# Differential attention of two batches taken out of its own stage: one beside the last exps, one beside the experts

## The chip, the cores and the metric

The kernel runs on one core of one Trainium2 chip. The metric is the device time of one execution in microseconds (us). The kernel before took 1091.72 us, the median of three runs (1090.41 to 1093.3).

## The reference, cut to what matters

The input is x with 8 batches of 512 tokens of width 128, in float32. Two blocks follow each other. Each normalizes its rows (layer norm), feeds the normalized rows to an attention and, in parallel, to a second layer, and adds both to x.

- Block 0: causal attention with 16 heads of width 8, beside a soft mixture of experts (64 slots for each of 8 experts).
- Block 1: *differential attention* beside a transformer layer of its own. That layer has a small causal attention over the batch index (the eight tokens at one position), a router that picks the best two of 8 experts for each token, at most 1280 tokens for each expert in order of arrival, and the experts (128 to 512 to 128 with GELU).

```
# differential attention of one batch, xn its normalized rows
q1, q2 = split(xn @ w_q12);  k1, k2 = split(xn @ w_k12);  v = xn @ w_v
a = softmax(q1 k1^T / sqrt(128)) - lam * softmax(q2 k2^T / sqrt(128))
out = a @ v;  out = out / rms(out) * (1 - 0.8)
x += out + transformer_layer(xn)
```

The order of arrival makes the router serial over the batches: the place of a token in its expert's list (its *rank*) counts all earlier tokens of that expert.

## The kernel before, in words

Names: a tile is 128 partitions wide; a batch is 4 tiles of 128 rows (NI is 4). PE multiplies matrices, DVE is VectorE, ACT is ScalarE, POOL is GpSimd, SP issues plain transfers. Each engine works its own queue in order. The order of PE, DVE, ACT and POOL follows the order in which the program is written out: `in_order` (L230) chains each engine's instructions up to the experts in that order.

The program has four stages.

1. **The soft experts of block 0** (L513 to L578), and then a start of the attention.
2. **The attention loop of block 0** (L1185 to L1228). A step `e_` is called a *third* here: one third of the causal score tiles of one group of 4 heads, 96 thirds (N3) in all, 12 to a batch. A third's work has two halves. `m_head` (L1035) makes scores for the row maximum (PE line L1042, DVE line L1052); `e_head` (L1066) makes the scores again and ACT takes the exp (L1075, L1080). `m_head` runs AHEAD (8) thirds in front of `e_head`, so in the last 8 thirds there is only `e_head`. After each third POOL masks the exps (L1085) and PE multiplies them with the values (`av`, L1100). A batch ends with `out_att`, `out_T` and `out_x` (L1111 to L1140), which add the attention to x.
3. **Differential attention**, `diff(range(NB))` (L1334), one batch after the other: four projections (`diff_qk`, L1253), the values (`diff_v`), and for each of 4 row tiles two score matmuls with max and exp (`diff_scores`, L1277, L1281, L1282), their difference (`diff_both`, L1295), transposes (`diff_T`) and the product with the values (`diff_out`, L1311). `diff_end` scales the rows on DVE and adds them to x, and `store` writes the batch to the output.
4. **The experts** (L1398). For each expert SP loads its 1280 rows (L1400), PE transposes them (L1418), multiplies (L1428), ACT does the GELU (L1431), PE multiplies again (L1435), DVE scales (L1441), and POOL issues ten indirect transfers (L1446), each of which adds 128 rows to the output. The additions of an expert wait until all those of the expert before have landed.

**Leads.** The transformer layer's attention and router for batch b are a generator, `lead(b)` (L665), started when `out_x(b)` is done. `step_leads` (L1169) advances each open lead by at most one step in each *slot* (a quarter of a third, or one step of `diff`). A lead's chain is: layer norm (`ln_stats`, `ln_apply`), its projection (L690), b+1 query products on POOL, each summed on DVE (L722, L716), an exp, b+1 value products on POOL, each added on DVE (L751, L760), the output projection (L782), a second layer norm, the router (L812 to L851, small operations going to and fro between DVE and POOL), the ranks (L858 to L877), and 8 indirect transfers on POOL that put the rows into the experts' lists (*puts*, L903). A lead may not begin its query products before the lead in front of it is done with its values (`after("sc", s_ - 1)`, L703). All puts of all leads must have landed before the first load of an expert's rows (L1401).

**Ranks.** PE adds up 9 small matmuls in one tile (L858 to L868): the counts of earlier batches (`seen`), the tokens above in the same tile (`tri`, once for each of two choices), and the whole tiles before it (`ones`, six times).

The lists of steps 3 and 4 use different PSUM pools; in stage 3 tag "d" has 3 buffers for the scores and "t" has 3, in stage 4 "t" has 2 (L1392).

Of the kernel before, what the change touches and what calls it, by code (L numbers as in the profile page):

```python
# [18 lines left out]
P = 128  # L19
# [6 lines left out]
def kernel(ctx: ExitStack, tc: tile.TileContext, a: dict, out: bass.AP):  # L26
# [203 lines left out]
    def in_order(start, end=None):  # L230

        free = mybir.DependencyInfo(mybir.DependencyClass.NoSync, mybir.DependencyReason.DATA)
        last = {}
        for ins in list(nc.cur_bb.bb.instructions)[start:end]:
            if ins.engine in engines:
                if ins.engine in last:
                    tc.add_manual_dep(ins, last[ins.engine], free, reason="order of the trace")
                last[ins.engine] = ins.name

# [348 lines left out]
    seen = const.tile([P, NE], F32, name="seen")  # L588

    def routing_in():  # L590
# [5 lines left out]
        nc.gpsimd.memset(seen, 0.0)  # L596
# [38 lines left out]
    def ln_stats(name, rows):  # L635
        stt = small.tile([P, 4, 6], F32, tag="bn_st", name=f"st_{name}")
        mv = small.tile([P, 4, 2], F32, tag="bn_mv", name=f"mv_{name}")
        for k, r in enumerate(rows):
            dve.bn_stats(out=stt[:, k, :], in_=r)
            dve.bn_aggr(out=mv[:, k, :], in_=stt[:, k, :])  # L640
            yield 1, "dve"
# [23 lines left out]
    def lead(s_):  # L665
# [37 lines left out]
        yield from after("sc", s_ - 1)  # L703
        sc = wt("sc", [NI * H, NB])
# [15 lines left out]
        for t in range(n):  # L720
# [3 lines left out]
            if len(behind) > BEHIND:  # L724
                yield 1, "dve"
                sum_q(*behind.pop(0))
# [22 lines left out]
        for t in range(n):  # L749
# [8 lines left out]
            if len(behind) > BEHIND:  # L758
                yield 1, "dve"
# [51 lines left out]
        for i in range(NI):  # L811
# [39 lines left out]
        pool.tensor_scalar(out=hot[:, 1], in0=off, scalar1=0.0, scalar2=None, op0=ALU.is_equal)  # L851
        yield 3, "pe"
# [5 lines left out]
        nc.tensor.matmul(  # L858
            pr, lhsT=ones, rhs=seen.unsqueeze(1).to_broadcast([P, NI, NE]), start=True, stop=False
        )  # L860
        for k in range(2):
            nc.tensor.matmul(pr, lhsT=tri, rhs=hot[:, k].rearrange("p i e -> p (i e)"), start=False, stop=False)
        for k in range(2):
            for i in range(NI - 1):
                nc.tensor.matmul(
                    pr[:, (i + 1) * NE :], lhsT=ones,
                    rhs=hot[:, k, i].unsqueeze(1).to_broadcast([P, NI - 1 - i, NE]),
                    start=False, stop=(k == 1 and i == NI - 2),  # L868
                )
# [4 lines left out]
        new = rtile("new", (NE,))  # L874
        dve.tensor_reduce(out=new, in_=hot.rearrange("p k i e -> p e (k i)"), axis=AX.X, op=ALU.add)
# [11 lines left out]
        pool.tensor_tensor(out=seen, in0=seen, in1=new, op=ALU.add)  # L887
# [10 lines left out]
        yield 3, "pool"  # L898

        for i in range(NI):  # L900
            m = s_ * NI + i
            for k in range(2):
# [8 lines left out]
                yield 1, "pool"  # L911
# [4 lines left out]
    with ExitStack() as at:  # L916
# [226 lines left out]
        AHEAD = 8  # L1143
# [20 lines left out]

        leads = []
# [3 lines left out]
        def step_leads(slot_, pe_free, pool_free, more):  # L1169
            room[0] = min(room[0] + more, more)  # L1170
            spare[0] = min(spare[0] + more * SPARE, CAPA * more)
            for r in list(leads):
                if slot_ < r[1] or (r[2] == "pe" and not pe_free) or (r[2] == "pool" and not pool_free):
                    continue
                if r[2] == "dve" and room[0] <= 0 or r[2] == "act" and spare[0] <= 0:
                    continue
                if r[2] == "pool":
                    pool_free = False
                nxt = next(r[0], None)
                if nxt is None:  # L1180
# [4 lines left out]
        for e_ in range(-AHEAD, N3 + 4):  # L1185
# [13 lines left out]
            for n in range(4):  # L1199
# [20 lines left out]
                if e_ < 0:  # L1220
                    next(rest, None)
                step_leads(4 * e_ + n, n == 1, n < 3, ROOM)
# [6 lines left out]

        in_order(first)  # L1230


    with ExitStack() as l1b:
# [9 lines left out]
        wka = l1b.enter_context(tc.tile_pool(name="wka", bufs=2, reuse_waits="tile"))  # L1243


        ascale = D ** (-0.25)
        OUT = (1.0 - LAMBDA_INIT) * math.sqrt(D)
        dd = {}

        def diff_qk(b):  # L1250
            for n, (w, c) in enumerate((("wq1", 0), ("wk1", 0), ("wq1", 1), ("wk1", 1))):
                pq = psum_t(f"pqk_{b}_{n}")
                nc.tensor.matmul(pq, lhsT=l1p[w][:, c * D : (c + 1) * D], rhs=xnT[:, b], start=True, stop=True)  # L1253
                dd["qk", b, n] = o = wka.tile([P, T], F32, tag=f"qk1_{n}", name=f"qk1_{b}_{n}")
                nc.scalar.activation(o, pq, AF.Identity, scale=ascale if w == "wq1" else 1.0)
                yield

        def diff_v(b):
            pv = psum_t(f"pv1_{b}")
            for i in range(NI):  # L1260
                nc.tensor.matmul(
                    pv[:, i * D : (i + 1) * D], lhsT=xnT[:, b, i * P : (i + 1) * P], rhs=l1p["wv1"], start=True, stop=True
                )
            dd["v", b] = v = wka.tile([P, NI, D], F32, tag="v1", name=f"v1_{b}")
            nc.scalar.copy(v.rearrange("p i d -> p (i d)"), pv)

        def diff_scores(b, i):

            u = f"{b}_{i}"
            nm = small.tile([P, 2], F32, tag="nm", name=f"nm1_{u}")  # L1270
            dd["ex", b, i] = ex = wka.tile([P, 2, T], F32, tag="ex1", name=f"ex1_{u}", bufs=4)
            if i == 0:
                dd["sm", b] = small.tile([P, NI, 2], F32, tag="sm1", name=f"sm1_{b}")
            sm = dd["sm", b][:, i]
            for k in range(2):
                sc = psum_t(f"s1_{u}_{k}", "d")
                nc.tensor.matmul(  # L1277
                    sc, lhsT=dd["qk", b, 2 * k][:, i * P : (i + 1) * P], rhs=dd["qk", b, 2 * k + 1],
                    start=True, stop=True,
                )  # L1280
# [212 lines left out]
```

## Time and profile before

| what | value |
|---|---|
| median of 3 runs | 1091.72 us |
| the profiled execution | 1097.12 us |
| its span, first to last instruction | 1095.4 us |
| PE / DVE / ACT / POOL busy | 91% / 60% / 50% / 51% of the span |
| mean granted TensorE clock | 0.941 |
| last `out_x` of block 0 ends (start of stage 3) | 732.1 us into the span |
| first load of an expert's rows issued | 900.0 us |
| first transposes of an expert's rows on PE | 915.2 us |
| first addition to the output issued | 929.1 us |
| last addition issued | 1089.6 us |

The profiled execution is 1.7 us longer than its span and 5.4 us longer than the median. A row of the table by stretches has, after its bounds, the length of the stretch, then the busy time and the number of instructions of PE, of its weight loads, of DVE, ACT and POOL, then the granted clock of PE (1.00 is full), the busy share of the DMA engines and what they moved. Busy PE is not the same as fast PE: at a granted clock of 0.50 the same matmuls take about twice as long and still count as busy. In the timeline a bracket shows how long the engine had been idle before an instruction and what ended the idle time.

### The profile page before, as it was taken

How to read it: one execution, taken by the hardware profiler on the slowest of the kernel's cores; microseconds unless marked ns; L12 is line 12 of the kernel's file. 1: busy time of each engine (PE TensorE's matmuls, PEld its weight loads, DVE VectorE, ACT ScalarE, POOL GpSimd, SP SyncE). 2: the span in 40 equal slices, each digit the busy share in tenths (PEclk: the TensorE clock that was granted, in tenths of full speed). 3: DMA queues.
4: the chain of work that ended last, by engine and by line, in shares of the span. 5: the costliest groups of instructions: out<-in, count | busy, mean ns of one | idle time of the engine just before them, and what ended most of it. 6: DMA issues, size and time to landing. Idle time of an engine off the chain costs nothing.

```text
span 1095.4 us, 19018 instructions
## 1 busy us (share of the span) xinstructions
PE 1000.8 (91%) x6838; PEld 639.9 (58%) x6838; DVE 661.9 (60%) x2134; ACT 551.4 (50%) x1263; POOL 559.7 (51%) x761
## 2 busy tenths in 40 slices
PE   6889899989899999999999999788978987999992
PEld 3457556866455555555556555354655655777772
DVE  6734543287677887788878689437786754222220
ACT  3566348352456676667465654526554753222220
POOL 3201000202143527675876787875877351777776
PEclk8999899999799999999999899759998998999996
DMA  8630000000000000000000000050000013342312
GB/s 249 149 91 1 1 1 1 1 1 1 1 1 2 1 2 2 20 2 1 17 7 1 21 19 4 1 171 1 20 11 20 20 44 94 49 67 40 29 15 25
DMA packets 49311, 32.99 MB, mean 30 GB/s; under 512 B 12232, under 2 KB 44275, under 8 KB 49216
## 3 DMA queue, kind: packets, MB, share of 16 engines
q1 hardware_dynamic: 34832, 24.80, 8.4%
q0 software_dynamic: 13568, 6.70, 4.5%
q8 instruction: 54, 0.88, 0.3%
q14 instruction: 41, 0.34, 0.1%
q10 hardware_dynamic: 816, 0.26, 0.1%
HBM read 17.56 MB, written 17.07 MB: 32 GB/s over the span
## 4 chain that ended last, share of the span: by engine, by line
PE 73%; POOL 10%; DVE 9%; issue 4%; ACT 3%; DMA 2%; POOLq 0%; DVEq 0%; ACTq 0%; SPq 0%
PE se L1075 11%; PE sm L1042 7%; PE pem L1435 7%; PE po L1100 7%; PE phm L1428 6%; PE lg_d L302 3%; PE s L1277 3%; PE pe L477 3%; PE psl L346 3%; PE lg_c L302 2%; PE pq L962 2%; PE pf L379 2%; PE ph L451 2%; POOL xs L903 2%; DVE junk L1052 2%
## 5 line engine op out<-in xcount | busy, mean ns | idle before, releaser
L1052 DVE CUSTOM_DVE_ANT_0 junk<-sm,cmask 128x128 f32<-128x128 f32 (+3 forms) x512 | 249.6, 488 | 82.2 <-PE sm L1042 29.3
L1080 ACT ACTIVATE pt<-se 128x384 f32<-128x384 f32 (+1 forms) x384 | 186.5, 528 | 175.1 <-PE se L1075 102.2
L1042 PE MATMUL sm<-kj,qT 32*128 32x256 f32 (+3 forms) x1024 | 229.9, 485 | 4.3 <-ACT kj L629 2.7
L1075 PE MATMUL se<-q,kj 32*128 32x512 f32 (+3 forms) x1024 | 212.0, 484 | 3.8 <-DVE q L616 3.6
L1075 PEld LDWEIGHTS se<-q,kj 32*128 32x128 f32 x1024 | 101.2, 192 | 83.1 <-issue 26.7
L1446 POOL DMA_INDIRECT out_dram<-es,to x80 | 124.2, 1552 | 48.0 <-issue 22.5
L1085 POOL TENSOR_SCALAR_AFFINE_SELECT pt<-pt 128x512 f32<-128x512 f32 (+1 forms) x96 | 79.3, 826 | 128.2 <-ACT pt L1080 127.8
L1042 PEld LDWEIGHTS sm<-kj,qT 32*128 32x128 f32 x1024 | 111.5, 190 | 20.6 <-DVE mcol L1052 6.5
L1100 PE MATMUL po<-pt,vpad 128*18 128x512 f32 (+3 forms) x1024 | 92.9, 460 | 9.2 <-POOL pt L1085 9.2
L1431 ACT ACTIVATE hTm<-phm 128x1024 f32<-128x1024 f32 (+1 forms) x48 | 42.2, 881 | 109.5 <-PE phm L1428 105.0
L1435 PEld LDWEIGHTS pem<-w,hTm 128*128 128x128 f32 x640 | 77.1, 192 | 16.8 <-ACT hTm L1431 12.1
L1435 PE MATMUL pem<-w,hTm 128*128 128x128 f32 x640 | 81.2, 278 | 0.5 <-ACT hTm L1431 0.2
L1428 PE MATMUL phm<-xeT,w 128*128 128x512 f32 (+1 forms) x192 | 75.2, 523 | 2.3 <-DVE xeT L1420 2.3
L1441 DVE TENSOR_SCALAR es<-pem,wt 128x128 f32<-128x128 f32 x80 | 22.9, 345 | 89.9 <-PE pem L1435 85.2
L1282 ACT ACTIVATE ex<-s,nm 128x512 f32<-128x512 f32 x64 | 43.8, 687 | 65.9 <-DVE nm L1281 65.3
L903 POOL DMA_INDIRECT xs<-l_z,sput x64 | 66.1, 1033 | 17.2 <-issue 16.3
L508 POOL TENSOR_TENSOR x_all<-x_all,bo_bc 128x512 f32<-128x512 f32 x8 | 10.2, 1277 | 121.8 <-DVE xn L266 121.8
L1277 PE MATMUL s<-qk,qk 128*128 128x512 f32 x128 | 65.4, 630 | 5.0 <-ACT ex L1282 5.0
L1281 DVE TENSOR_REDUCE nm<-s 128x1 f32<-128x512 f32 x64 | 42.7, 682 | 20.0 <-PE s L1277 19.1
L1100 PEld LDWEIGHTS po<-pt,vpad 128*18 128x18 f32 x1024 | 21.0, 99 | 52.3 <-issue 21.6
L1311 PEld LDWEIGHTS po<-v,dT 128*128 128x128 f32 x256 | 35.2, 204 | 20.9 <-ACT sqj L1315 10.2
L1428 PEld LDWEIGHTS phm<-xeT,w 128*128 128x128 f32 x192 | 33.6, 191 | 23.1 <-issue 17.2
(264 smaller groups left out, 1906.4 us busy)
## 6 DMA issues: line engine op xcount, KB each, us to landing
xs<-cmask SPq DMA_DIRECT2D x1, 5280.0 KB
xe<-xs SPq DMA_DIRECT2D x8, 660.0 KB
x_all<-in_L_attn_x_dram SPq DMA_DIRECT2D x8, 256.0 KB, 4.2
w<-in_L_ffn_w_dram SPq DMA_DIRECT2D x1, 2048.0 KB, 9.1
w<-in_L_ffn_moe_w_dram SPq DMA_DIRECT2D x1, 2048.0 KB
out_dram<-x_all SPq DMA_DIRECT2D x8, 256.0 KB, 2.2
out_dram<-es,to POOLq DMA_INDIRECT x80
xs<-l_z,sput POOLq DMA_INDIRECT x64
```

Of the source, the lines that this page charges most:

```text
L302: nc.tensor.matmul(lg, lhsT=lhs(k), rhs=rhs, start=True, stop=True)
L903: put = nc.gpsimd.indirect_dma_start(out=xs, out_offset=bass.IndirectOffsetOnAxis(ap=sput[:, k, m : m + 1], axis=0), in_=z2[:, i], in_offs ...
L1042: nc.tensor.matmul(sc[:, o : o + w], lhsT=st["qT", b][rr, i * P : (i + 1) * P], rhs=st["k", b, j][rr, :w], start=True, stop=True,)
L1052: nc.vector.tensor_tensor_reduce(out=junk[:, :w], in0=sc[:, o : o + w], in1=cmask[:, 512 - w : 512], scale=-1.0, scalar=BIG, op0=ALU.add, ...
L1075: nc.tensor.matmul(sc[:, o : o + w], lhsT=st["k", b, j][rr, c * P : (c + 1) * P], rhs=st["q2", b, (g % G) // 2][rr, c * P : T], start=True ...
L1080: nc.scalar.activation(st["pt", g, k][:, r, :o], sc[:, :o], AF.Exp)
L1085: nc.gpsimd.affine_select(out=pt[:, :, :n, :P], in_=pt[:, :, :n, :P], pattern=[[0, 4], [0, n], [1, P]], compare_op=ALU.is_ge, fill=0.0, ba ...
L1100: nc.tensor.matmul(po[32 * r : 32 * r + 2 * PW, c * P : T], lhsT=vpads[b % 3][:, c, at_ : at_ + 2 * PW], rhs=pt[:, r, o : o + w], start=(c ...
L1277: nc.tensor.matmul(sc, lhsT=dd["qk", b, 2 * k][:, i * P : (i + 1) * P], rhs=dd["qk", b, 2 * k + 1], start=True, stop=True,)
L1428: nc.tensor.matmul(ph[:, k, :w], lhsT=w1_1[:, e, hc * P : (hc + 1) * P], rhs=xeT[:, :w], start=True, stop=True)
L1435: nc.tensor.matmul(pe[:, k * D : (k + 1) * D], lhsT=hT[:, hc, k * P : (k + 1) * P], rhs=w2_1[:, e, hc, :], start=(hc == 0), stop=(hc == NH ...
L1446: back = nc.gpsimd.indirect_dma_start(out=out_rows, out_offset=bass.IndirectOffsetOnAxis(ap=to[:, c : c + 1], axis=0), in_=es[:, c], in_of ...
```

## The change

It has six parts.

- **Ranks.** POOL adds the two choices (`both`) and keeps running counts for every tile (`seen` gets NT + 1 entries); PE then needs 2 matmuls for a batch in place of 9, and DVE one sum less.
- **AHEAD** goes from 8 to 9.
- **Leads in stage 3** take steps whose pause is one slot and whose kind is "act" (or "row", a new name for the layer norm's sums) together in one slot; and `sc` has two buffers, so that a lead's query products wait only for the lead two in front. "put" and "sum" are further names of kinds.
- **The early batch.** Batch 0's `diff` runs in the attention loop from third 88 on, one step in each slot, with tiles borrowed from the loop (`home`), and its products in SBUF. Its row tiles use two score buffers in turn.
- **The late batch.** Batch 7's `diff` runs in stage 4, two steps in each group of row tiles (three groups to an expert) of the first four experts, between the GELU and the second matmuls. Its x is stored before the experts; its attention is scaled in SBUF and added to the output by one POOL transfer of the whole batch after expert 4's additions, which it awaits and which expert 5's additions await.
- **Stage 3** keeps batches 1 to 6, and `behind` chains the experts' instructions on each engine behind the last one of stage 3.

```diff
-    seen = const.tile([P, NE], F32, name="seen")
+    seen = const.tile([P, NT + 1, NE], F32, name="seen")
...
-        yield from after("sc", s_ - 1)
-        sc = wt("sc", [NI * H, NB])
+        yield from after("sc", s_ - 2)
+        sc = wt("sc", [NI * H, NB], bufs=2)
...
+        both = rtile("both")
+        pool.tensor_tensor(out=both, in0=hot[:, 0], in1=hot[:, 1], op=ALU.add)
+        for i in range(NI):
+            m = s_ * NI + i
+            pool.tensor_tensor(out=seen[:, m + 1], in0=seen[:, m], in1=both[:, i], op=ALU.add)
         yield 3, "pe"
...
-        nc.tensor.matmul(
-            pr, lhsT=ones, rhs=seen.unsqueeze(1).to_broadcast([P, NI, NE]), start=True, stop=False
-        )
-        for k in range(2):
-            nc.tensor.matmul(pr, lhsT=tri, rhs=hot[:, k].rearrange("p i e -> p (i e)"), start=False, stop=False)
-        for k in range(2):
-            for i in range(NI - 1):
-                nc.tensor.matmul(
-                    pr[:, (i + 1) * NE :], lhsT=ones,
...
+        nc.tensor.matmul(pr, lhsT=ones, rhs=seen[:, ns].rearrange("p i e -> p (i e)"), start=True, stop=False)
+        nc.tensor.matmul(pr, lhsT=tri, rhs=both.rearrange("p i e -> p (i e)"), start=False, stop=True)
...
-        AHEAD = 8
+        AHEAD = 9
...
+        EARLY = (0,)
+        LATE = (NB - 1,)
+        APART = EARLY + LATE
...
+            if tag == "ex1":
+                t = wkp.tile([P, NG, S], F32, tag="sq", name=name) if i % 2 == 0 else wkp.tile([P, NI, 2 * H, S], F32, tag="qk", name=name).rearrange("p i h s -> p (i h) s")
...
+                sc = psum_t(f"s1_{u}_{k}", "d" if b not in APART else "t")
...
+            if b in APART:
+                nc.vector.tensor_copy(to, po)
...
                 nxt = next(r[0], None)
+                while nxt and nxt[0] == 1 and nxt[1] in at_once:
+                    nxt = next(r[0], None)
...
+                if e_ >= N3 - 8:
+                    if n % 1 == 0:
+                        next(early, None)
                 step_leads(4 * e_ + n, n == 1, n < 3, ROOM)
...
-        run = diff(range(NB))
+        run = diff(range(len(EARLY), LATE[0]))
...
-                step_leads(slot_, True, True, 9.0)
+                step_leads(slot_, True, True, 9.0, ('act', 'row'))
                 slot_ += 1
+        for b in LATE:
+            store(b)
         in_order(tail)
+        experts = len(nc.cur_bb.bb.instructions)
...
+        late = diff(LATE)
         for e in range(NE):
...
+                if e < 4:
+                    for _ in range(2):
+                        next(late, None)
                 pe = psum_o(f"pem_{e}_{c0}")
...
+            if e == 4:
+
+                for _ in late:
+                    pass
+                add = nc.gpsimd.dma_start(
+                    out=out[LATE[0]].rearrange("(i p) d -> p i d", p=P),
+                    in_=dd["po", LATE[0]].rearrange("p (i d) -> p i d", i=NI), accum_op=ALU.add,
+                )
+                for name in backs[e + 1]:
+                    tc.add_manual_dep(add.ins, name, sync, reason="a row is read and written by each addition")
+                backs[e + 1] = [add.ins.name]
+
+        behind(tail, experts)
```

The order in which the changed program issues its instructions: on PE the early batch lies between the scores of third 88 and those of third 94; on POOL, between the last mask and the last put, there are 32 puts, 15 query products, 16 value products and the small operations of leads 5 to 7; on ACT the table of functions is loaded 12 times more during experts 0 to 2, since the late batch's exps fall between the GELUs.

## Prediction

> **What bounds the kernel now.** I read the busy time by stretches first. Its columns are named under the table of the profile.
>
> ```profile
> 680.00:690.00 10.00, 7.81 (x74) 3.50 (x72) 8.91 (x28) 6.71 (x16) 7.41 (x13) 1.00 0.00 0
> 690.00:700.00 10.00, 6.17 (x52) 2.65 (x56) 2.73 (x3) 7.96 (x19) 9.75 (x12) 0.98 0.00 0
> 700.00:731.00 31.00, 28.49 (x134) 18.16 (x126) 11.33 (x30) 5.53 (x14) 20.49 (x35) 0.50 0.35 111
> 745.00:762.00 17.00, 13.42 (x56) 8.26 (x57) 11.61 (x24) 12.32 (x31) 5.13 (x8) 0.90 0.00 0
> 762.00:845.00 83.00, 73.32 (x354) 46.81 (x353) 60.70 (x130) 42.08 (x122) 68.52 (x97) 0.96 0.06 17
> 845.00:900.00 55.00, 53.81 (x277) 36.56 (x278) 37.16 (x93) 37.64 (x109) 24.12 (x47) 0.97 0.07 20
> 900.00:916.00 16.00, 8.98 (x51) 7.58 (x49) 7.26 (x27) 6.06 (x20) 1.95 (x4) 0.79 0.56 144
> 916.00:1076.00 160.00, 154.77 (x916) 116.46 (x916) 43.14 (x130) 43.85 (x51) 112.66 (x74) 1.00 0.29 41
> ```
>
> Four things are to be seen. At 690 to 700 PE is busy for 6.17 of 10 us, and from 700 to 731 it is granted half its clock: it looks busy, but does about half the work. From 762 to 845 POOL is the fullest that it gets in stage 3 (its short pauses between puts not counted). From 845 to 900 PE is the bound. From 916 to 1076 PE is full, and POOL too, once its pauses are counted.
>
> The timeline says what stands behind these rows: the stall ahead of the half clock, the stall at 900, and how the additions run.
>
> ```profile
> 699.70 0.63 PE L1100 MATMUL po<-pt,vpad 128*18 128x256 f32 x4 [3.28 <-POOL pt L1085]
> ...
> 904.70 0.17 DVE L1405 TENSOR_SCALAR first<-xe 128x10 f32<-128x10 f32 x1 [7.12 <-DMA xe<-xs]
> ...
> 929.11 1.67 POOL L1446 DMA_INDIRECT out_dram<-es,to  x1 [10.12 <-DVE es L1441]
> 931.09 1.57 POOL L1446 DMA_INDIRECT out_dram<-es,to  x1 [0.30 <-issue]
> ...
> 949.51 1.55 POOL L1446 DMA_INDIRECT out_dram<-es,to  x1 [2.02 <-DVE to L1412]
> ```
>
> The second line is an expert's first DVE instruction, queued ahead of differential work; it waits for the load and holds DVE for 7.12 us. The additions leave every 1.86 us (1.55 and a pause of 0.30), and between two experts POOL waits about 2 us for the landing: expert 1 starts at 949.5, expert 2 at 969.9, expert 5 at 1031.3, expert 7 at 1072.9, so 20.4 us an expert. PE needs 19.7 (its second matmuls start at 963.64, 1003.05 and 1042.46: 39.4 for two). Both limits nearly coincide.
>
> The list of waits, for stage 3 (735 to 915), names what PE waited for:
>
> ```profile
> PE dT_p L141 <- DVE ex L1295: 6.7, 4, 2.1
> PE po L1311 <- ACT sqj L1315: 6.4, 2, 6.0
> PE s L1277 <- ACT ex L1282: 5.0, 2, 4.0
> ```
>
> **The unit that is moved.** One batch of differential attention costs PE, at full clock by the chain of 855 to 900: 4 projections of 0.86, values 0.89, 8 scores of 0.86, 4 transposes of 0.63, 4 products of 0.89, together 17.3 us. DVE needs 11.4 us for it (42.7 + 26.1 + 9.5 + 4.8 + 7.9 us over 8 batches, lines L1281, L1295, L1292, L1291, L1328), ACT about 12.
>
> **Ranks: -5 us.** In the loop the 12 instructions of L865 take 1.32 us, 0.11 each; a batch has 18 (each matmul is two), the change leaves 4. That is 14 x 0.11 = 1.5 us of PE a batch. Four ranks lie in the loop ahead of third 88, where PE is busy for 20.00 us of 20 in most stretches: up to 6.2 us. What is late next is the POOL mask (PE waited 5.0 us for it between 280 and 680), and POOL gets four more operations a batch, of about 0.25 us with their gap (L887's kind). I take 5, bounds 0 and 6.2. The second buffer of `sc` moves POOL work forward in the loop; POOL is busy there for 5 to 19 us of 20, so I count nothing.
>
> **AHEAD 9: 0.** Four m_heads move from the loop to its start. PE: 4 x 0.23 us, hidden nowhere, but taken out of a full loop. DVE: 4 heads of 0.42 + 0.29 and gaps, 3.6 us at the start, where PE already waits for DVE (3.3 us for `q`). The new m_head is queued behind that `q`, not ahead of it. Bounds: -3.3 (the wait is covered) and +3.6 (all of DVE's work late).
>
> **The tail of the loop: +5.** Third 88 starts at about 680 and stage 3 at 732, 52 us. At full clock PE's work in it is 14 us (680 to 700) and about 16 of the 28.5 busy us at half clock (a set of 4 scores takes 0.86 us at 679 and 1.58 at 701), so 30. The early batch adds 17.3; the shorter rank takes 1.5, and the order of lead 5's projection puts another 1.5 into stage 3: 44.5 us of PE work. To this comes the closing chain (copy, transposes, division, transposes, copy, `pw`, addition: 0.59 + 0.63 + 0.78 + 0.63 + 0.59 + 1.2 + 0.7, 5 us) and I take 7 us for stalls: 57. The batch fills the time in which PE stood and ran slowly. Bounds: 48 (no stall) and 70 (half of the tail at half clock). One stall is built in: with two score buffers, the exp of row tile 2 waits on ACT for the transposes of row tile 0, and behind it in ACT's queue stand the block 0 exps, for whose buffers (7) PE waits next.
>
> [...]
>
> **Stage 3: -45.** Before it takes 183 us (732.1 to 915.2). After, two limits:
>
> - PE: 6 batches of 17.3 are 104, the PE work of leads 5 to 7 is 14 (transposes 0.63, `pp` 0.89, `pl` 0.79, the projection of lead 7 1.8, three ranks of 0.45): 118 us.
> - POOL, from the last mask to the last put: 32 puts each 1.28 us after the other (41), 15 query products of 1.25 (19), 16 value products of 1.14 (18), layer norm operations 10, additions 3 x 1.27 (4), routers 3 x 3.9, new counts 3 x 1.4, weights and slots 3 x 3.1, row scales of four batches 4 x 1.75: together 124 us, of which some 11 lie ahead of `out_x(7)`.
>
> So both stand near 115 us, and each waits for the other in its queue (a rank waits for POOL, products for DVE). DVE has about 6 x 11.4 plus leads, 110 us. From 762 to 845 POOL's busy time and its pauses between 16 puts (0.30 each) make 73 of 83 us, 88%. I take this rate: 124 / 0.88 = 141 us, less 11 is 130 to the last put. Then the load lands (4.6 us, 900.04 to the DVE line above) while PE ends batch 6, whose last work is late by the rank of lead 7; the row scales and the first rows' copy add 3: 138. The stall of 900 to 907 goes, since `behind` keeps the experts' DVE work behind stage 3. Bounds: 123 (124 - 11 and the load, no stalls) and 150 (80%).
>
> **Experts: +21.** The late batch gives PE 17.3 us over four experts: 19.7 + 4.3 = 24.0 us an expert, above POOL's 20.4. Expert 4's first addition comes 14 + 1.7 (two projections ahead) + 4 x 24.0 = 112 us after the stage's start; from the same event to the end the trace has 1095.4 - 1011.0 = 84.4 us. Then POOL is the bound again and nothing is made good. The new transfer of the whole batch stands between experts 4 and 5 with its own issue and landing; no row shows one. Below: one indirect issue and landing, 1.55 + 2.0; above: four of them, 4 x 1.86 + 2 = 9.4. I take 5, nearer to the single issue, because the plain store of as many bytes lands in 2.2 us. So 112 + 84.4 + 5 = 201 us, where it took 180.2. ACT's 12 loads of 1.28 us lie beside 3.6 us of second matmuls each time and cost nothing; if that cover fails, they are 15 us. PSUM tag "t" has two buffers here, which the late scores share with the rows' transposes; I count it in the upper bound. Bounds: +15 (PE's idle 5 us absorb a part) and +40.
>
> [...] The trace's loads last 1.28 us. [...]
>
> **Sum.** -5 + 0 + 5 - 45 (183 to 138) + 21 = -24 us. Against the profiled execution that is 1097.1 - 24 = 1073; the median lies 5.4 lower, so 1067 (1067.7).
>
> **Rivals.**
>
> - *Both limits of stage 3 are met and the clock holds.* Leads 5 to 7 now overlap, so POOL may never starve: stage 3 at 125, the tail at 50. Then -6 - 2 - 58 + 21 = -45: 1046. Against it: POOL waited in stage 3 for ACT and DVE (8.0 us for one exp). Chance 0.15.
> - *The early batch stalls the exps.* The ACT wait above empties PE, and the half clock stays: with 44.5 us of work, half of it at half clock, and the stalls, the tail takes 78 where I took 57. Then 1088 to 1090. For it: the clock did not return for 31 us before. Chance 0.12, and its spread reaches both sides of no change.
> - *Lead 7 keeps its length (slower).* In the trace it runs from 731 to its last put at 898.6, 167 us. If that is latency from step to step and not POOL's work, stage 3 cannot end before 167 + 8 = 175, and the late batch only lengthens the experts: -5 + 5 - 8 + 21 = +13, 1104. It decides from a lead of 155 us on. For it: the lead has over 40 steps that go to and fro between POOL and DVE. Against it: from 845 to 900 POOL was busy for 24 of 55 us and the lead followed PE's slots, of which there are now fewer. Chance 0.13.
>
> **How the numbers follow.** The forecast, 1055 to 1082, has 0.60. A change of 0.3% (3.3 us) is about what a measurement of this kernel can tell from none. Faster: 0.60 + 0.15 + 0.05 = 0.80; same 0.04; slower 0.03 + 0.13 = 0.16. The range, 1042 to 1092, holds the forecast, the fast case and most of the second rival, and leaves out the third.
>
> **What would show each step.** PE's granted clock between third 88 and stage 3 near 1.00 (the tail); from the last `pw` to the first transposes of an expert's rows 130 to 145 us, POOL busy over 85% (stage 3); no DVE wait for `xe` among differential work; second matmuls of experts 0 to 3 every 24 us and later every 19.7; the additions of experts 5 to 7 every 20.4 us; one gap of about 7 us ahead of expert 5's. The prediction is wrong if PE waits in stage 3 for lead 7's rank, if the tail shows 0.50, or if the big transfer holds POOL for over 10 us.

## The result, and the profile after

The changed kernel is slower. It took 1098.8 us, the median of 4 runs (1097.09 to 1101.7), where the kernel before took 1091.52 beside it (1090.41 to 1093.3): a ratio of 1.007, interval [1.0047, 1.0092]. The forecast was 1067, and 1042 to 1092 as its range.

The two profiled executions took 1097.12 (before) and 1097.09 us (after), so the traces differ by nothing where the medians differ by 7.3 us: the profiled execution of before lies 5.6 us above its median, that of after 1.7 below. Where in before's trace these 7 us lie isn't shown; its mean granted clock is 0.941, where 17 executions beside the first set of experiments had 0.944 to 0.949 at 1087.1 to 1095.0 us, so more time at half clock is the likeliest place. Two executions of the same code are up to 7 us apart at third 88 (673.2 in the kernel that is called neither below, 680.4 in rank_late57, which differs from it only later), so a few us of every time in the loop are chance. From there on, stages that two kernels share repeat within 2 us in most runs, and the reading goes by these.

I cut both traces at the same four points: the start of third 88's mask, the end of the last `pw` of block 0 (the product with the output weights, PE's last work in `out_x`), the end of the last put of lead 7, and the first transposes of an expert's rows.

| stage | before | after | forecast of the change | measured |
|---|---|---|---|---|
| up to third 88's mask | 681.3 | 674.1 | -5 | -7.2 |
| tail: third 88's mask to last `pw` | 50.1 | 59.8 | +5 | +9.7 |
| stage 3: last `pw` to first expert's rows | 183.9 | 160.7 | -45 | -23.2 |
| experts to the end | 180.2 | 200.8 | +21 | +20.6 |

The largest error is stage 3, by 22 us. In sum the stages were forecast at -24 us and came out at 0 between the two traces. The other 7 us of the miss are the forecast's last step, which took the median of the changed kernel 5.4 us below its profiled execution; it lies 1.7 above. The times of the stages are read from the traces at the starts and ends of these instructions. Busy time by stretches, of the changed kernel (columns as under the table of the profile before):

```profile
674.00:720.00 46.00, 45.99 (x248) 23.70 (x247) 21.22 (x45) 26.31 (x69) 21.42 (x42) 1.00 0.01 2
720.00:734.00 14.00, 8.31 (x53) 5.24 (x52) 3.40 (x9) 2.60 (x6) 11.51 (x17) 0.66 0.42 126
745.00:762.00 17.00, 13.73 (x43) 7.19 (x42) 15.02 (x34) 9.97 (x27) 10.97 (x16) 0.90 0.00 0
762.00:843.00 81.00, 67.62 (x307) 43.05 (x307) 61.74 (x123) 42.67 (x121) 69.73 (x102) 0.92 0.04 13
843.00:885.00 42.00, 37.32 (x187) 25.32 (x186) 24.41 (x64) 24.39 (x73) 23.55 (x47) 0.92 0.09 25
885.00:895.00 10.00, 5.05 (x22) 4.79 (x23) 2.17 (x7) 1.41 (x6) 2.13 (x7) 0.66 0.85 227
916.00:1076.00 160.00, 154.46 (x907) 115.74 (x906) 50.59 (x146) 63.06 (x85) 109.92 (x74) 1.00 0.29 40
```

The half clock of 700 to 731 is gone: PE is busy for all of 674 to 720 at 1.00, and only the end of the tail is slow (0.66 from 720 to 734). But PE is busy for 54.3 us in the two rows together, where I had counted 44.5 of work and some 2.5 for PE's part of the closing chain. In stage 3 POOL is as full as forecast only in the middle: 69.73 of 81 us, before its pauses between puts. From 745 to 762 it is busy for 10.97 of 17 us, and from 843 to 885 for 23.55 of 42. That last stretch is lead 7 alone. Its POOL timeline:

```profile
842.54 0.97 POOL L905 DMA_INDIRECT xs<-l_z,sput  x1 [0.30 <-issue]
...
849.55 0.23 POOL L127 TENSOR_SCALAR rs_l<-mv_l 128x4 f32<-128x4 f32 x1 [4.04 <-DVE mv_l L625]
...
860.26 0.24 POOL L835 TENSOR_TENSOR r_lg<-r_lg,r_most 128x32 f32<-128x32 f32 x1 [7.51 <-DVE cc L1232]
...
884.05 0.97 POOL L905 DMA_INDIRECT xs<-l_z,sput  x1 [0.30 <-issue]
```

After lead 6's last put (842.54) nothing of the leads but lead 7's output projection, second norm, router, rank and 8 puts is left for POOL, beside the row scales of two batches, and these steps go to and fro with DVE and PE: 42.5 us from the start of that put to the end of the last. And the list of waits for the same stage (735 to 905) shows what stood at the head of PE's queue:

```profile
PE prank L873 <- POOL seen L866: 9.5, 3, 4.1
PE dT_p L141 <- DVE ex L1236: 6.9, 3, 4.5
PE a1T_p L141 <- DVE l_at L625: 3.3, 1, 3.3
```

The rank is what the prediction named as a sign against it. In before PE waited 0.5 us for ranks in stage 3. At the end of the stage the expert's first DVE instruction no longer waits for its load, as forecast, but DVE waits all the same, for POOL's row scales (the first line below; the second is the expert's):

```profile
896.78 1.12 DVE L1279 SCALAR_TENSOR_TENSOR x_all<-po,ri,x_all 128x128 f32<-128x128 f32 x4 [7.50 <-POOL ri L129]
897.83 0.16 DVE L1449 TENSOR_SCALAR first<-xe 128x10 f32<-128x10 f32 x1
```

The experts went as forecast. The additions of experts 0 to 4 start at 910.2, 935.6, 959.6, 982.5 and 1007.1, 22.9 to 25.4 us apart and 24.2 in the mean, where 24.0 was forecast. The timeline of POOL between experts 4 and 5:

```profile
1023.76 1.55 POOL L1493 DMA_INDIRECT out_dram<-es,to  x1 [0.30 <-issue]
1027.08 1.39 POOL L1507 DMA_DIRECT2D out_dram<-po  x1 [1.77 <-DMA out_dram<-es,to]
1032.55 1.63 POOL L1493 DMA_INDIRECT out_dram<-es,to  x1 [4.08 <-DMA out_dram<-po]
```

From the end of the last addition (1025.31) to the next is 7.24 us, with the transfer of the whole batch between them. ACT's 13 loads of its table of functions in this stage, 1.28 us each, cost PE next to nothing: between 910 and 1090 PE waits 1.7 us for ACT in all.

### The profile page after: what moved, and what is told of

Same layout as the page of the kernel before. It is cut to its first block, busy times and chain, and to the rows that moved or that the text cites. A ratio compares the mean times of both kernels' runs of the same rounds, so it can differ in the third digit from the quotient of the medians.

```text
span 1095.4 us, 18827 instructions
## 1 busy us (share of the span) xinstructions
PE 991.4 (91%) x6726; PEld 604.5 (55%) x6726; DVE 669.5 (61%) x2134; ACT 569.1 (52%) x1275; POOL 567.7 (52%) x794
## 4 chain that ended last, share of the span: by engine, by line
PE 66%; POOL 13%; DVE 11%; issue 5%; ACT 3%; DMA 1%; POOLq 0%; DVEq 0%; ACTq 0%
PE se L1077 12%; PE pem L1482 6%; PE phm L1472 6%; PE po L1102 6%; PE sm L1044 4%; PE lg_d L311 3%; DVE junk L1054 3%; PE pe L486 3%; PE s L1218 3%; PE psl L355 3%; POOL xs L905 3%; PE pf L388 2%; PE pq L964 2%; PE lg_c L311 2%; PE ph L460 2%
## 5 line engine op out<-in xcount | busy, mean ns | idle before, releaser
L1077 PE MATMUL se<-q,kj 32*128 32x512 f32 (+3 forms) x1024 | 219.2, 472 | 4.0 <-DVE mcol L1054 3.5
L1077 PEld LDWEIGHTS se<-q,kj 32*128 32x128 f32 x1024 | 104.1, 186 | 91.2 <-DVE mcol L1054 24.3
L1044 PEld LDWEIGHTS sm<-kj,qT 32*128 32x128 f32 x1024 | 111.8, 190 | 24.5 <-DVE mcol L1054 10.2
L1102 PE MATMUL po<-pt,vpad 128*18 128x512 f32 (+3 forms) x1024 | 89.7, 446 | 10.5 <-POOL pt L1087 10.5
L1475 ACT ACTIVATE hTm<-phm 128x1024 f32<-128x1024 f32 (+1 forms) x48 | 41.6, 881 | 77.1 <-PE phm L1472 77.0
L905 POOL DMA_INDIRECT xs<-l_z,sput x64 | 66.9, 1046 | 16.6 <-issue 15.0
L1218 PE MATMUL s<-qk,qk 128*128 128x512 f32 x128 | 68.5, 645 | 4.0 <-ACT ex L1223 3.0
L1488 DVE TENSOR_SCALAR es<-pem,wt 128x128 f32<-128x128 f32 x80 | 22.9, 344 | 75.7 <-PE pem L1482 75.7
L1102 PEld LDWEIGHTS po<-pt,vpad 128*18 128x18 f32 x1024 | 20.6, 97 | 60.6 <-issue 21.1
L731 POOL TENSOR_TENSOR l_prod<-l_qkv 128x512 f32<-128x512 f32 x36 | 45.5, 1277 | 0.1
```

The lines of the kernel that those rows point to most:

```text
L905: put = nc.gpsimd.indirect_dma_start(out=xs, out_offset=bass.IndirectOffsetOnAxis(ap=sput[:, k, m : m + 1], axis=0), in_=z2[:, i], in_offs ...
L1044: nc.tensor.matmul(sc[:, o : o + w], lhsT=st["qT", b][rr, i * P : (i + 1) * P], rhs=st["k", b, j][rr, :w], start=True, stop=True,)
L1077: nc.tensor.matmul(sc[:, o : o + w], lhsT=st["k", b, j][rr, c * P : (c + 1) * P], rhs=st["q2", b, (g % G) // 2][rr, c * P : T], start=True ...
L1102: nc.tensor.matmul(po[32 * r : 32 * r + 2 * PW, c * P : T], lhsT=vpads[b % 3][:, c, at_ : at_ + 2 * PW], rhs=pt[:, r, o : o + w], start=(c ...
L1218: nc.tensor.matmul(sc, lhsT=dd["qk", b, 2 * k][:, i * P : (i + 1) * P], rhs=dd["qk", b, 2 * k + 1], start=True, stop=True,)
```

## The experiments

Twelve kernels were run, each five rounds against the kernel before, whose median was 1092.24, 1092.55 and 1093.88 in the three sets of four. The table has what all of them gave. Where an experiment is written as an edit, it is one of the changed kernel unless it names the kernel before. The ratio is to the kernel before, with its interval; "lead 7" is from the last `pw` to its last put, "rest" from there to the first transposes of an expert's rows, and the two make up stage 3. The stages are those of one execution each.

| kernel | batches in stage 3 | ratio | tail | lead 7 | rest | stage 3 | experts |
|---|---|---|---|---|---|---|---|
| before | 8 | 1 | 50.1 | 167.3 | 16.6 | 183.9 | 180.2 |
| after | 6 | 1.0070 [1.0047, 1.0092] | 59.8 | 151.1 | 9.6 | 160.7 | 200.8 |
| no_late | 7 | 0.9975 [0.9960, 0.9990] | 59.9 | 150.1 | 22.2 | 172.3 | 179.1 |
| no_early | 7 | 0.9941 [0.9923, 0.9959] | 40.1 | 149.2 | 22.2 | 171.4 | 199.3 |
| neither | 8 | 0.9907 [0.9889, 0.9924] | 37.9 | 150.7 | 38.7 | 189.5 | 178.8 |
| ranks_ahead | 8 | 0.9930 [0.9911, 0.9950] | 40.3 | 175.7 | 15.4 | 191.1 | 178.6 |
| ranks | 8 | 0.9987 [0.9968, 1.0007] | 45.2 | 170.4 | 16.7 | 187.0 | 178.9 |
| ahead9 | 8 | 0.9935 [0.9911, 0.9959] | 42.1 | 173.8 | 15.5 | 189.3 | 180.3 |
| early_fours | 6 | 0.9972 [0.9952, 0.9991] | 50.5 | 150.2 | 9.6 | 159.7 | 199.0 |
| best1 | 7 | 0.9881 [0.9859, 0.9903] | 50.4 | 150.1 | 22.2 | 172.3 | 179.1 |
| best1_nb | 7 | 0.9901 [0.9882, 0.9921] | 50.5 | 150.8 | 25.3 | 176.1 | 178.6 |
| lead7_short | 6 | 0.9911 [0.9889, 0.9932] | 52.2 | 129.5 | 22.9 | 152.4 | 199.7 |
| rank_later | 8 | 1.0146 [1.0117, 1.0176] | 52.6 | 154.7 | 38.8 | 193.5 | 182.3 |
| rank_late57 | 8 | 0.9935 [0.9912, 0.9958] | 40.2 | 150.9 | 37.5 | 188.3 | 181.1 |

### What the two moved batches are worth: no_late, no_early, neither

The theory after the result: stage 3 is as long as lead 7's chain, so a batch that leaves it gives back less than it costs elsewhere (L). The rival: the stage is the sum of its work, and gives back the full price of a batch (T).

```diff
# no_late
-        LATE = (NB - 1,)
+        LATE = ()
-        run = diff(range(len(EARLY), LATE[0]))
+        run = diff(range(len(EARLY), NB))
# no_early
-        EARLY = (0,)
+        EARLY = ()
# neither: both
```

> The changed kernel with the late batch put back as the seventh batch of stage 3 and no big transfer; everything else stays. Theory L (stage 3 of the changed kernel is as long as lead 7's chain of steps, 149.5 us from its start to its last put plus 10, and PE has some 40 us of slack in its 159 us): the batch put back costs stage 3 between 5 and 12 us, the experts give back 20.6, so 1098.8 - 20.6 + 8 = about 1086. Theory T (stage 3 is bound by the sum of its work, and a batch costs there what it costs elsewhere, 17 to 20 us): stage 3 near 177, 1096 to 1098.

> The changed kernel with the early batch put back as the first of seven in stage 3; everything else stays. The stretch from third 88 to stage 3 was 52 us in the kernel before and 63 in the changed one, so about 11 us come back there. Theory L: stage 3 grows by 5 to 12 us from 159, total 1093 to 1100, so that the early batch is worth about nothing. Theory T: stage 3 grows by 17 to 20 us, total 1104 to 1108.

> The changed kernel with all eight batches in stage 3; shorter ranks, AHEAD 9, the leads' new pace and the chaining of the experts behind stage 3 stay. Theory L: the two moves are a net loss. The loop keeps its 8 to 10 us, the tail returns to 52, the experts to 180, and stage 3 stays at 183 at most: 1080 to 1085. Theory T: stage 3 grows by 35 to 40 us to about 196, 1098.8 - 11 - 20.6 + 37 = 1104.

Measured: 1089.06, 1086.37 and 1081.64 us. No_late and neither lie nearer to L's totals, no_early lies below both. Without the two batches the rest of the change is a gain of 0.93%. The early batch alone (no_late against neither) costs 0.0068 x 1092 = 7 us, the late one alone (no_early) 4 us, both 18 us: 7 us more than the two by themselves, where each of these differences is known to some 3 us.

The stages say why, and both theories hold a part. The tail costs 20 to 22 us more with the early batch (59.8 against 40.1, 59.9 against 37.9), not the 11 that no_early's expectation took. The late batch costs the experts 20 to 22. Stage 3 gives 17 to 18 us back when the eighth batch leaves it (189.5 to 172.3 or 171.4), which is T, and 11 to 12 when the seventh does (to 160.7), which is L. The rows of the stretches up to lead 7's last put and behind it show how. First neither (eight batches), then no_late (seven), then after (six):

```profile
711.00:862.00 151.00, 124.06 (x539) 76.92 (x539) 110.17 (x233) 80.01 (x220) 111.31 (x172) 0.92 0.11 34
862.00:900.00 38.00, 35.62 (x197) 24.79 (x196) 24.57 (x59) 25.77 (x77) 5.34 (x14) 1.00 0.29 76
```

```profile
734.00:884.00 150.00, 125.28 (x535) 77.16 (x534) 108.42 (x232) 79.37 (x219) 110.46 (x171) 0.91 0.11 34
884.00:906.00 22.00, 19.61 (x122) 14.67 (x121) 14.49 (x35) 14.45 (x45) 4.16 (x11) 1.00 0.46 118
```

```profile
734.00:885.00 151.00, 126.33 (x556) 79.16 (x555) 109.96 (x235) 80.60 (x225) 111.40 (x171) 0.91 0.11 35
```

Up to the last put the three are the same: 150 us, in which PE is busy for 124 to 126 and POOL for 110 to 111. What is left of the batches then follows: 38 us and 22 us at full clock, or 10 us. The 10 us hold the load of the first rows and the last batch's end. The order of the program ties the batches to the leads' slots, and the leads take 150 us whether six or eight batches are to be fitted in. What sets these 150 us isn't told apart here, the leads' own steps or the PE work that the order puts between them.

PE's side of stage 3 can be split in three. The table has it by the busy time and by the stretches in which each trace grants half the clock (0.50). A set of four scores of one form takes 0.92 us in before at 679.40, at full clock, and 1.65 at 701.12, at 0.50. As an estimate from this, half of PE's busy time in these stretches is counted as lost, and the rest of the busy time is its work at full clock.

| kernel | batches | stage 3 | PE idle | lost at half clock | work at full clock |
|---|---|---|---|---|---|
| before | 8 | 183.9 | 22.7 | 11.5 | 149.7 |
| neither | 8 | 189.5 | 29.3 | 11.0 | 149.2 |
| no_late | 7 | 172.3 | 27.1 | 13.5 | 131.7 |
| after | 6 | 160.7 | 29.6 | 16.1 | 115.0 |

Each batch takes the 17 us of work with it that the prediction had priced. With the second one, PE's idle time and its loss at half clock grow by 5 us, and the stage gives back that much less.

### Which part brought the gain: ranks, ahead9, ranks_ahead

```diff
# ahead9: the kernel before with
-        AHEAD = 8
+        AHEAD = 9
# ranks: the kernel before with the shorter ranks of the change
# ranks_ahead: both; written from the changed kernel, with EARLY = (), LATE = (),
-        sc = wt("sc", [NI * H, NB], bufs=2)
+        sc = wt("sc", [NI * H, NB])
-                step_leads(slot_, True, True, 9.0, ('act', 'row'))
+                step_leads(slot_, True, True, 9.0)
# and without behind(tail, experts)
```

> The kernel before with the shorter ranks and AHEAD 9 alone: one sc buffer, the old pace of the leads, no chaining of the experts, all eight batches in stage 3. By the times of the masks these two parts are worth 8 to 10 us up to third 88, and the ranks of leads 4 to 7 another 4 to 6 us of PE work in stage 3: 1077 to 1083 against the 1091.5 of the kernel before. If the gain of the loop comes from the second sc buffer or the early batch instead, it stays within 1088 to 1092.

> The kernel before with the shorter ranks alone (AHEAD 8). Both together took 7.2 us off the time, 8 us up to third 88's mask and 10 us in the tail, where the half clock is gone. The instruction counts give the ranks 1.5 us of PE for each of the four in the loop: by them 1086 to 1088, with the half clock of the tail unchanged. If the ranks also end the half clock of the tail: 1076 to 1082.

> The kernel before with AHEAD 9 alone. The masks of thirds 6 to 36 come 3 us earlier in the changed kernel, ahead of any rank, so this part should be worth about 3 us: 1088 to 1090. If it is the ninth third that ends the half clock of the tail (fewer scores for PE to wait for there is no longer true, since m_heads end one third earlier and PE has less to do at the end): the clock would be no better, and the time 1090 to 1094.

Measured: 1085.07, 1090.48 and 1086.33 us. The shorter ranks can't be told from no change (0.9987, interval to 1.0007), AHEAD 9 gives 0.65%, both together 0.70%. None of the expectations had it that way: the ninth third is worth twice what I took at most, and the ranks a part of theirs. The tail of each of the three is 5 to 10 us shorter than before, but stage 3 is 3 to 7 us longer, so that a part of what is gained ahead of it is lost again there. The half clock is a part of the shorter tail: the long stretch at 0.50 lasts 37.5 us in before (699.5 to 737.1), 23.9 in ahead9 (698.8 to 722.7) and 17.1 in ranks (696.6 to 713.7), by the changes of the granted clock in the traces. It isn't shown which wait of the loop the ninth third takes away.

Against ranks_ahead, neither has the new pace, the second `sc` and the chaining of the experts. These cut lead 7 from 175.7 to 150.7 us, and yet stage 3 only goes from 191.1 to 189.5: with eight batches it isn't lead 7 that ends it.

### Why the tail took 20 us for a batch of 17: early_fours

```diff
-                    if n % 1 == 0:
+                    for _ in range(4 if n == 3 else 0):
                         next(early, None)
```

> The changed kernel with the early batch's steps moved: four of them after the fourth head of each third, in place of one after each head. Theory O (the scores of neighbouring heads use 32 rows each and run on PE at the same time; a full-height score of the early batch between two of them takes that away, 80 score matmuls take 22 us of PE against 13.8 without the early batch): the same 80 take about 14 us again, the stretch from third 88's mask to the last product of block 0 goes from 59.8 to about 51, total near 1090. Rival P (the early batch costs its own 17 us of PE time and its waits on two score buffers, and the order does not matter): 59 to 62 us, total 1097 to 1101. Four steps together also leave less time between an early score and the exp that frees its buffer, which can take a part of the gain back.

Measured: 1088.7 us, 0.0098 x 1092 = 11 us less than the changed kernel, and the tail at 50.5. The groups of PE from 672.1 to 734 have the scores of block 0 in these lines (L1077), and in two of them those of the early batch (L1218), with the busy time and the mean of one behind the bar; first after, then no_early, then early_fours:

```profile
L1077 PE MATMUL se<-q,kj 32*128 32x256 f32 (+3 forms) x82 | 22.5, 445 | 0.0
L1218 PE MATMUL s<-qk,qk 128*128 128x512 f32 x16 | 9.0, 645 | 0.0
```

```profile
L1077 PE MATMUL se<-q,kj 32*128 32x256 f32 (+3 forms) x80 | 13.8, 504 | 0.0
```

```profile
L1077 PE MATMUL se<-q,kj 32*128 32x256 f32 (+3 forms) x82 | 12.4, 444 | 0.0
L1218 PE MATMUL s<-qk,qk 128*128 128x512 f32 x16 | 7.5, 599 | 0.0
```

The mean of one is 445 and 444 ns in the first and the third, but 82 of them take 22.5 us of PE in one and 12.4 in the other: 82 times the mean is 36 us, so that on average 1.6 of them run at a time in the first and 2.9 in the third. (The mean of no_early, 504 ns, holds matmuls at half clock, which costs its tail 7.7 us by the next table.) The timeline shows it. In after a head's score, then a score of the early batch, and so on:

```profile
685.95 1.12 PE L1077 MATMUL se<-q,kj 32*128 32x512 f32 x2
687.00 1.13 PE L1218 MATMUL s<-qk,qk 128*128 128x512 f32 x2
```

In early_fours, the scores of two heads (four instructions) take the time of one:

```profile
682.13 1.13 PE L1077 MATMUL se<-q,kj 32*128 32x512 f32 x4
```

A head's score uses 32 of 128 rows (the 32*128 of its lines). The four matmuls of two neighbouring heads take 1.13 us in early_fours, and one head's two take 1.12 in after with a full-height matmul on either side: no matmul of another head runs beside them. Theory O held (12.4 us for about 14, a tail of 50.5 for 51), rival P fell. There is a second loss beside the lost overlap: the early batch's 16 score matmuls take 9.0 us between heads and 7.5 in a row. What makes it isn't shown.

Even in whole sets the early batch makes the tail 10 to 13 us longer than without it. The split of PE's time, made as for stage 3, says what it costs and what it fills:

| kernel | tail | PE idle | lost at half clock | work at full clock |
|---|---|---|---|---|
| before | 50.1 | 8.5 | 14.6 | 27.0 |
| neither | 37.9 | 8.8 | 4.6 | 24.5 |
| no_early | 40.1 | 8.2 | 7.7 | 24.1 |
| early_fours | 50.5 | 6.2 | 2.7 | 41.6 |
| after | 59.8 | 5.7 | 2.9 | 51.2 |

In whole sets the batch adds 17 us of work, its price, and fills 5 to 7 us of idle time and half clock; head by head it adds 27.

### Whether lead 7 ends stage 3 with six batches: lead7_short

```diff
-        n = s_ + 1
+        n = s_ + 1 if s_ < NB - 1 else 3
```

> early_fours (six batches in stage 3, the late batch beside the experts) with lead 7 attending to the first 3 batches only, so that 5 of its 8 query products and 5 of its 8 value products, with their sums, are left out: 5 x 1.25 + 5 x 1.14 = 12 us of POOL and as much on DVE. Theory L (with six batches stage 3 ends with lead 7's last put plus 10 us): lead 7 goes from 150 to about 138 and stage 3 from 159.7 to between 148 and 154, where PE's own work (189.5 less two batches of 17.5) stops it; total 1078 to 1083. Theory T (PE's queue alone sets the stage): stage 3 stays within 3 us, total 1086 to 1089.

The kernel leaves out five query and five value products of lead 7, so it computes something else and serves for its time alone. Measured: 1084.03 us. Lead 7 took 129.5 us, 20.7 less than in early_fours, for 12 us of POOL work left out; by the same estimate as above the PE work inside it fell too, from 113.5 to 95.1 us. Stage 3 took 152.4, 7.3 less. Behind lead 7's last put there are now 23 us in place of 9.6, and PE is busy for 19.7 of them:

```profile
862.00:885.00 23.00, 19.73 (x121) 14.65 (x120) 14.86 (x36) 14.35 (x46) 3.63 (x10) 1.00 0.44 114
```

So with six batches two limits stand close together: lead 7's chain at 160 us, and PE at 152, which by the same estimate are 115 of work, 26 of idle time and 11 lost at half clock. The gain of 0.61% against early_fours is of the size of stage 3's; its interval ([0.9889, 0.9932] against [0.9952, 0.9991]) is apart from it.

### Whether PE's waits for the rank cost stage 3: rank_later, rank_late57

```diff
-        yield 3, "pe"       # ahead of the rank's matmuls
+        yield 8, "pe"       # rank_later
+        yield 3 if s_ < 5 else 8, "pe"       # rank_late57
```

> The kernel with all eight batches in stage 3 (the one called neither, 1081.6) with the rank's two matmuls issued 8 slots behind POOL's counts in place of 3. PE waited 9.5 us in stage 3 for the counts, 3 times, at the head of its queue. Theory Q (stage 3 is PE's queue: work and the waits at its head): those waits go, stage 3 shortens by 5 to 9 us, 1073 to 1077. Theory L (lead 7's chain decides): lead 7 grows by about 5 us, and the time stays or grows, 1081 to 1086.

> The kernel with all eight batches in stage 3 (neither, 1081.6) with the rank's matmuls 8 slots behind POOL's counts for leads 5 to 7 alone, so that the loop keeps its order. rank_later, which moved the ranks of all leads, lost 9 us up to third 88 and 15 us in the tail, and its stage 3 took 193.5 us against 189.5. Theory Q (waits at the head of PE's queue add to stage 3): 9.5 us of waits go, stage 3 at 181 to 186, total 1074 to 1079. If other waits take their place, as the list of waits of rank_later has it (6.4 us for lead sums, 5.8 for exps): 1081 to 1086.

Measured: 1109.89 us for rank_later, where all leads' ranks moved, and 1087.64 for rank_late57, where only those of stage 3 did. PE waited 1.8 us for the rank in stage 3 in place of 9.5, but stage 3 took 188.3 us where neither took 189.5. Other waits came in their place, as the list of waits of rank_late57 (714 to 910) has them:

```profile
PE dT_p L141 <- DVE ex L1236: 6.0, 4, 2.2
PE z2T_p L141 <- ACT l_z L638: 4.5, 2, 2.3
PE a1T_p L141 <- DVE l_at L625: 3.9, 2, 2.1
PE s L1218 <- ACT qk L1196: 3.5, 2, 2.9
```

The 9.5 us were in neither and in after alike; in ranks_ahead, with the old pace of the leads, this wait was 3.2 us. Theory Q falls: what PE doesn't wait for at one place, it waits for at the next. The ratio (0.9935, neither 0.9907) isn't apart from neither's. That rank_later is 28 us slower than neither comes from the loop and the tail for the most part (third 88 at 682.2, the tail at 52.6 us where neither has 37.9); which step of the leads did that there wasn't followed up.

### The best of the parts: best1, best1_nb

```diff
# best1: LATE = (), and the early batch's steps by fours
# best1_nb: best1 without
-        behind(tail, experts)
```

> Shorter ranks, AHEAD 9, the new pace of the leads, the early batch with four steps after the fourth head, and no late batch. From the stages measured so far: third 88's mask at 674.5, tail 50.5 (early_fours), stage 3 with seven batches 172 (no_late), experts 179 (no_late): span 1076, 3 us under the version with all eight batches in stage 3. Theory O with the slope of stage 3 (17 us a batch down to seven batches): 1076 to 1079 us. If the early batch is worth nothing even in whole sets, because the tail grows by 12.6 us and stage 3 gives back less: 1081 to 1085.

> The kernel called best1 without the chaining of the experts' instructions behind stage 3. If the stall of an expert's first DVE instruction among the last differential work, 7 us in the kernel before, still costs time, this is 3 to 7 us slower than best1. If DVE has room there, the two are within 2 us.

Measured: 1080.93 and 1084.23 us. best1 is faster than the kernel before by 1.2% (0.9881) and than the changed one by 1.9%, by the two ratios. Against neither (0.9907) its interval overlaps: that the early batch in whole sets is a gain isn't shown, and neither is the gain by `behind` (3.3 us by the medians, with stage 3 at 176.1 in place of 172.3). What is shown is that the changed kernel is faster than both without its late batch, with or without the early one (no_late, neither, best1).

## Why the prediction was wrong

- **What bounds the kernel.** Read rightly for the loop and the experts. For stage 3 it failed: POOL's 88%, from 83 us in the middle in which two leads overlap, was put on all of lead 7's span. There are stretches at both ends in which POOL waits (10.97 of 17 us and 23.55 of 42).
- **The unit.** The price of a batch was right: 17 us of PE work at full clock left stage 3 with each, by the estimate above. In its sum the transposes stand at 0.63 us, their time from start to end; from start to next start before's lines have 0.43 (855.97 to 856.40), which makes 16.5 us.
- **Ranks -5, AHEAD 0.** Together near: -7.2 us up to third 88, and a tail that is 10 us shorter without the early batch. Alone, the ranks gave 0.13% at an interval that holds no change, and AHEAD 9 gave 0.65%, 7 us, outside its bounds of -3.3 and +3.6. I had counted only what the moved `m_head`s cost, and not what one more third between the two halves does for the waits of the loop and its end.
- **Tail +5.** 59.8 us where I had 57, inside the bounds, and the clock at 1.00 up to 720. But that the number came near is in part luck, since two errors offset each other. The tail's own work was put too high: 30 us, of which the shorter rank and lead 5's projection take 3, where the tail without the batch has 24. And the early batch was put too low: 17.3 us for 27. Block 0's scores take 22.5 us of PE with it and 13.8 without; I took the price of heads that run side by side for an order in which each stands alone. What the batch was to fill was smaller too: the other parts leave a tail of 37.9 to 40.1 us with some 13 to 16 us of idle time and lost clock, where before had 23.
- **Stage 3 -45.** This is the step that failed: 183 to 138, measured 160.7. The sum divides POOL's work by a rate of 88%. The work was about right (113 us were forecast to the last put), the rate was not: from the last `pw` to lead 7's last put POOL had 111.4 us of work and 7 of pauses in 151 us, 78%. "Both stand near 115 us" left out that a lead is a chain that goes to and fro between the engines; lead 7 took 149 to 151 us with six, seven and eight batches in the stage. PE's 118 us of work were right as well (115.0), but the forecast left 20 us beside them, and no term of it stood for the half clock: PE's idle time was 29.6 us and its loss at half clock 16.1, together 46 where before had 34. Of the 22 us that were missing, 8 are lead 7's chain beyond the 152 us of lead7_short. The other 14 are in PE's idle time and half clock there; which of these could be had isn't shown, and one wait that was taken out (rank_late57) came back as others.
- **Experts +21.** Right in size and mechanism: 200.8 us for 201, 24.2 us an expert for 24.0, one gap of 7.24 us for about 7, POOL's period afterwards, and next to no cost of the table loads (PE waited 1.7 us for ACT in all).
- **The rivals.** The third, "lead 7 keeps its length", came nearest: 1104 for 1098.8. It had 0.13 and lay outside the range. Its chain did shorten (167.3 to 151.1; from ranks_ahead to neither, by the new pace and the second `sc`, 25 us), but the stage still ends with it. It named 155 us as the length from which a lead decides; at 151 it decided already. The second rival, the early batch that stalls the exps, had the place right (the tail) and the mechanism wrong: the ACT wait that it starts from is there (4.3 us, an exp of the early batch behind the transposes), but PE waited 3.4 us for masks in the whole tail, and its clock stayed at 1.00 to 720.

In one sum: each moved batch costs 20 to 22 us where it went. The first to leave stage 3 gives 17 to 18 back, the second 11 to 12.

## What to carry to other kernels

Before work is moved out of a stage, ask what the stage does when the work is gone. If a chain of steps on other engines runs through it, take the length at which that chain ran there as the floor until a run shows it shorter, and the price that the stage pays back for each piece until then. Split the bounding engine's time into work, idle time and time lost at half clock: the work leaves with the piece, the other two need not (here 17 us of work left with the second batch, and the other two grew by 5). Cost the new place as the rest of the change leaves it, not as the old profile shows it, since another part may already have closed the gap that was to be filled. Matmuls of few rows that run side by side are a set: put what is to go between them behind the whole set (82 matmuls of 32 rows took PE 12.4 us here in whole sets and 22.5 with the early batch's between the heads). A table of stages from one execution of each kernel is good to some us only: before's profile lay 5.6 us off its median.

## What the hardware showed that was not expected

- Scores of 32 rows: two heads' four matmuls take 1.13 us, one head's two take 1.12 when a full-height matmul stands on either side. The full-height ones lose as well: 16 take 9.0 us between heads and 7.5 in a row.
- The stretch at half clock at the end of the loop isn't a fixed price: 37.5 us in before, 23.9 in ahead9, 17.1 in ranks. PE was busy for 20.00 us from 700 to 720 in before and stayed at 0.50. In after the stretch is gone at 674 to 720 and comes as 0.66 at 720 to 734, where PE is busy for 8.31 of 14 us.
- In stage 3 the clock falls to half again and again, mostly for 3.4 or 6.8 us: 34 of after's 160.7 us are at half clock, 26 of before's 183.9.
- A load of ACT's table of functions between two ACT instructions took 1.31 us in all (from the end of one at 924.34 to the start of the next at 925.65 in after), of which the load is 1.28.
- One POOL transfer that adds a whole batch (512 rows of 128) to the output took 1.39 us to issue and 4.08 more until the next addition could start; additions of 128 rows mostly take 1.55 us each and 0.30 between them.
- The loop's first mask starts between 284.6 and 287.6 us in the twelve traces with AHEAD 9, so that kernels differ by 3 us before the parts that were compared begin; early_fours (284.7) and lead7_short (287.6) differ only in lead 7.
